# The KAN's input product in narrow pieces with copies by transfers, and the rotated query by transfers between partitions

## The chip, the core and the metric

The kernel runs on one core of a Trainium2 chip. The metric is the time of one execution on the device in microseconds; of several runs the median is taken. TensorE is called PE here, VectorE DVE, ScalarE ACT, GpSimd POOL, and SP is the engine that issues most transfers.

## What is computed

The input `x` is 16 batches (rows) of 512 tokens of 128 numbers. Two layers are applied. The first is a macaron layer of half a KAN feed-forward, attention, and half a KAN again; the second is half a mixture of experts, a linear recurrence, and half a mixture of experts again. What matters here is the first layer:

```python
# KAN: 64 input features, each with 16 hidden units of its own
s = jnp.einsum('btd,dm->btm', x, Win) + bin_
h = jax.nn.relu(s[..., None] * W1 + b1)
g = jnp.einsum('btmh,mh->btm', h, W2) + b2
out = jnp.einsum('btm,md->btd', g, Wout) + bout
...
# attention: 16 query heads of 8 numbers, 4 key heads, causal
q = q * cos + rotate_half(q) * sin
k = k * cos + rotate_half(k) * sin
...
x = x + 0.5 * kan(layernorm(x)); x = x + attn(layernorm(x)); x = x + 0.5 * kan(layernorm(x))
```

`rotate_half` swaps the two halves of a head's 8 numbers and negates one. The KAN runs twice for each batch, 32 times in all, and the query projection 16 times.

## The kernel before

**The order is written out by hand.** PE, ACT, DVE and POOL run their instructions in the order in which the program emits them (L222). The emission goes in turns. A batch b has a period of 44 turns (4 groups of heads by 11 banks, `TURNS`, L1182). In each turn the main work takes one step of `weights(b)` (L699: scores again, exp on ACT at L715, a causal mask on POOL at L717) and one of `maxima(b + 1)` (L638: scores on PE at L652, their row maxima on DVE at L657 and L662). Beside it, side work is emitted as far as the room of the turn allows (`MOST`, L234): `outputs` (L723, the product with the values at L738), `stage_in(b + 4)` (the first KAN and `attn_in`), `stage_out(b - 1)` (output product, second KAN, `gated`), and in later batches the routing. A piece of side work is a generator; each `yield` passes it to the next turn. PSUM tiles of the main work turn through 5 banks (L627), those of side work through 2 (`bank`, L259). Before batch 0 there is a ramp in which `filling[0]` is true and nothing is paced. After batch 15 the experts run (`experts`, L960), 3 turns for each of 256 jobs. SP is not in this hand-written order: its queue is laid out by the framework, near the order of emission, and it issues strictly in that queue's order, waiting at the head of it.

**The KAN** (`kan`, L347). The normalised input is transposed to `xT` (128 features by 512 tokens). Its input product is needed 4 times, since four hidden units are worked on at a time, one on each group of 32 partitions. The weights `win` hold each half (32 of the 64 features) 4 times, so that one product of 128x512 for a half (L356) makes the 4 copies at once; ACT copies each of the two results from PSUM to SBUF (L359). Then 8 ReLUs follow on ACT (L375, v = 0 to 3 for each half), and 8 narrow products of 32 output rows each (L385), which land in 4 groups of 32 partitions of one bank.

**The query** (`attn_in`, L435). `wq` gives the query, and `wqr`, its columns with the halves of each head swapped, gives the rotated query by a second product. DVE multiplies one with cos and one with signed sin (L444, L450), POOL adds them (L465). Three bf16 parts are made (`parts`, L406), written to DRAM (L425) and read back spread over partitions (L514); keys go the same way (L432, L508). `maxima` of that batch reads them first.

Of the kernel before, what the change touches and what calls it, by code (L numbers as in the profile page):

```python
# [8 lines left out]
F32 = mybir.dt.float32  # L9
# [29 lines left out]
LATE = 28  # L39
EP = 5  # L40
# [8 lines left out]
def tile_macaron(  # L49
# [55 lines left out]
    with ExitStack() as ph:  # L105
# [5 lines left out]
        hp = ph.enter_context(tc.tile_pool(name="p1_h", bufs=8))  # L111
# [66 lines left out]
        wq = cst.tile([D, NH, HD], F32, name="wq")  # L178
        nc.sync.dma_start(out=wq, in_=wq_in.rearrange("k (h d) -> k h d", d=HD))
# [6 lines left out]
        nc.sync.dma_start(out=rope, in_=rope_in)  # L186
# [8 lines left out]
        wqr = cst.tile([D, NH, HD], F32, name="wqr")  # L195
# [47 lines left out]
        def take(**work):  # L243

            for e, w in work.items():
                room[e] -= w
# [10 lines left out]
        held, kan_held, hurry = [0], [0], [False]  # L257
# [10 lines left out]
        def freed():  # L268
            held[0] -= 1
# [77 lines left out]
        def kan(b):  # L347

            _, xT = yield from norm(x[b])
            sk = []  # L350
            for half in range(2):
                while half and kan_held[0]:
                    yield
                kan_held[0] |= half
                ps = yield from bank([P, S], F32, "ps_s", 0.9)
                nc.tensor.matmul(ps, lhsT=win[:, half, :, :].rearrange("d i m -> d (i m)"), rhs=xT,  # L356
                                 start=True, stop=True)
                sh = (w1p if half else w2p).tile([P, S], F32, name=f"kan_s{half}")
                later.append(lambda sh=sh, ps=ps: nc.scalar.copy(sh, ps))  # L359
                yield  # L360
                take(act=0.6)
# [36 lines left out]
            for c in range(NT):  # L398
                nc.tensor.matmul(po[:, c, :], lhsT=gT[:, bass.ts(c, P)], rhs=wout, start=True, stop=True)  # L399
            later.append(lambda: nc.vector.tensor_add(x[b], po, x[b]))  # L400
# [20 lines left out]
        def spread(part, heads, name):  # L421

            scr = tc.dram_tile([3, HD, heads, S], BF16, name=name)
            for i in range(3):
                nc.sync.dma_start(out=scr[i].rearrange("d h t -> h d t"), in_=part[:, i, :])  # L425
            return scr
# [8 lines left out]
        def attn_in(b, st):  # L435
# [3 lines left out]
            tb = w1p.tile([P, S], F32, name="rope_b", tag="yT")  # L439
# [3 lines left out]
            nc.tensor.matmul(pa, lhsT=wq.rearrange("k h d -> k (h d)"), rhs=xT, start=True, stop=True)  # L443
            later.append(lambda: nc.vector.tensor_mul(ta, pa, rope[:, 0, :]))  # L444
            yield
            take(dve=0.7)
            freed()
            pb = yield from bank([P, S], F32, "ps_pb", 0.9)
            nc.tensor.matmul(pb, lhsT=wqr.rearrange("k h d -> k (h d)"), rhs=xT, start=True, stop=True)
            later.append(lambda: nc.vector.tensor_mul(tb, pb, rope[:, 1, :]))  # L450
            yield
            take(dve=0.7)
            freed()
# [10 lines left out]
            yield from need(pool=1.25)  # L464
            nc.gpsimd.tensor_tensor(ta, ta, tb, ALU.add)  # L465
# [18 lines left out]
            st["va"] = va  # L484
            if paced[0]:
                yield
# [17 lines left out]
            N = 3 * HD  # L504
            while taken[0] < NR * (b - NKP + 1):
                yield
# [34 lines left out]
        def prepare():  # L541
# [25 lines left out]
            centered(psc[:, 0, :], wq.rearrange("k h d -> k (h d)"))  # L567
# [4 lines left out]
            nc.vector.tensor_copy(wqr[:, :, 0:hh], wq[:, :, hh:HD])  # L572
            nc.vector.tensor_copy(wqr[:, :, hh:HD], wq[:, :, 0:hh])
# [196 lines left out]
        def stage_out(b, st):  # L770
            while len(st["out"]) < NR:
                yield
            if paced[0]:
                yield
                yield
            yT = yield from turned(st["y"].rearrange("p c r g d -> p c (r g d)"), "yT", w1p)
            po = yield from bank([P, NT, D], F32, "ps_o", 0.9)
            for c in range(NT):
                nc.tensor.matmul(po[:, c, :], lhsT=yT[:, bass.ts(c, P)], rhs=wo, start=True, stop=True)
            later.append(lambda: nc.vector.tensor_add(x[b], po, x[b]))  # L780
# [530 lines left out]
```

## Time and profile before

| | |
|---|---|
| median of 3 runs | 1580.87 us (1578.59 to 1582.71) |
| the profiled execution | 1578.82 us, of which the profile's span is 1577.0 us |
| granted TensorE clock, mean | 0.985 |
| batch periods 0 to 15 | from 108.5 us to 907.7 us of the span |
| length of the periods of batches 4 to 8 | 54.1, 48.7, 53.8, 48.7, 53.8 us |
| input product L356, 64 products in 128 records | PE, 654 ns a record |
| its copies L359 | ACT, 64 of 587 ns |
| second query product L449, 16 products in 32 records | PE, 628 ns a record |

An fp32 product appears as two records. Matmuls overlap in the pipeline, so the duration of a record is longer than what a product costs; the cost is read from the start of one group of products to the start of the next. Periods were found from the records of L715, of which there are 44 in each. A row of the profile's waits names who waited, for whom, how many microseconds in all, how often, and the longest. In the rows that split the span into stretches, the columns are the stretch, its length, and then for PE, PE's weight loads, DVE, ACT and POOL the busy time (and the count of instructions), then the granted clock, the share of DMA time and GB/s.

### The profile page before, as it was taken

How to read it: one execution, taken by the hardware profiler on the slowest of the kernel's cores; microseconds unless marked ns; L12 is line 12 of the kernel's file. 1: busy time of each engine (PE TensorE's matmuls, PEld its weight loads, DVE VectorE, ACT ScalarE, POOL GpSimd, SP SyncE). 2: the span in 40 equal slices, each digit the busy share in tenths (PEclk: the TensorE clock that was granted, in tenths of full speed). 3: DMA queues.
4: the chain of work that ended last, by engine and by line, in shares of the span. 5: the costliest groups of instructions: out<-in, count | busy, mean ns of one | idle time of the engine just before them, and what ended most of it. 6: DMA issues, size and time to landing. Idle time of an engine off the chain costs nothing.

```text
span 1577.0 us, 33209 instructions
## 1 busy us (share of the span) xinstructions
PE 1480.0 (94%) x11889; PEld 1044.6 (66%) x11905; DVE 1085.1 (69%) x3574; ACT 960.5 (61%) x1852; POOL 923.8 (59%) x1439
## 2 busy tenths in 40 slices
PE   5679999999999999999999899999999999999997
PEld 2334454445445454444444489999998999999997
DVE  5587877878788788888888245865579665753333
ACT  3455767778788777777776865444454444544443
POOL 2535545556655564556454766667666666767773
PEclk8889999999999999999999999999999999999999
DMA  5220110122111210221031113222332233333332
GB/s 136 78 62 29 58 53 14 49 59 60 32 37 54 60 52 14 56 61 41 26 91 53 52 45 71 58 61 70 73 72 61 71 73 62 81 65 68 68 68 61
DMA packets 107467, 92.89 MB, mean 59 GB/s; under 512 B 23469, under 2 KB 95862, under 8 KB 107062
## 3 DMA queue, kind: packets, MB, share of 16 engines
q1 hardware_dynamic: 84464, 67.67, 15.0%
q0 software_dynamic: 21584, 22.89, 7.8%
q8 instruction: 94, 1.54, 0.4%
q14 instruction: 71, 0.58, 0.1%
q10 hardware_dynamic: 1254, 0.20, 0.1%
HBM read 59.20 MB, written 35.45 MB: 60 GB/s over the span
## 4 chain that ended last, share of the span: by engine, by line
PE 78%; DVE 11%; ACT 4%; issue 2%; POOL 1%; DMA 1%; SPq 1%; ACTq 0%; DVEq 0%; POOLq 0%
PE ps_h L1025 14%; PE ps_y L1038 14%; PE ps_av L738 9%; PE ps_st L712 7%; PE ps_sc L652 6%; PE acc L989 5%; DVE below L657 4%; PE ps_kg L385 4%; PE ps_s L356 3%; PE ps_t L336 3%; ACT pt L715 2%; PE ps_x L954 2%; PE ps_g L799 2%; ACT kan_h L375 1%; PE ps_ko L399 1%
## 5 line engine op out<-in xcount | busy, mean ns | idle before, releaser
L715 ACT ACTIVATE pt<-ps_st 128x512 f32<-128x512 f32 (+1 forms) x704 | 378.9, 567 | 127.2 <-PE ps_st L712 115.4
L717 POOL TENSOR_SCALAR_AFFINE_SELECT pt<-pt 128x128 f32<-128x128 f32 (+2 forms) x704 | 252.5, 367 | 315.2 <-ACT pt L715 309.1
L657 DVE CUSTOM_DVE_ANT_0 below<-ps_sc,causal 128x512 bf16<-128x512 f32 (+1 forms) x512 | 315.5, 616 | 102.1 <-PE ps_sc L652 86.2
L934 POOL DMA_INDIRECT xg<-xnd,tokI x256 | 253.0, 988 | 80.8 <-issue 36.4
L1027 ACT ACTIVATE mo<-ps_h 128x512 f32<-128x512 f32 x256 | 152.8, 597 | 217.3 <-PE ps_h L1025 215.2
L1025 PE MATMUL ps_h<-xin,mw 128*128 128x128 f32 x2048 | 272.5, 276 | 0.0
L1038 PE MATMUL ps_y<-mw,mo 128*128 128x128 f32 x2048 | 270.8, 275 | 0.0
L712 PE MATMUL ps_st<-qp,kp 128*128 128x512 bf16 (+3 forms) x1008 | 247.3, 301 | 24.7 <-DVE topped L657 18.6
L652 PE MATMUL ps_sc<-kp,qp 96*128 96x512 bf16 (+3 forms) x1024 | 255.0, 303 | 10.5 <-ACT pt L715 6.6
L1025 PEld LDWEIGHTS ps_h<-xin,mw 128*128 128x128 f32 x2048 | 250.3, 192 | 12.4 <-issue 9.9
L1038 PEld LDWEIGHTS ps_y<-mw,mo 128*128 128x128 f32 x2048 | 249.4, 192 | 1.0 <-DVE ye L1035 0.8
L712 PEld LDWEIGHTS <-kp 128*128 128x128 bf16 x1024 | 94.9, 100 | 191.3 <-issue 171.5
L375 ACT ACTIVATE kan_h<-kan_s,rbias,kw 128x512 f32<-128x512 f32 x256 | 207.5, 820 | 0.0
L1055 POOL DMA_INDIRECT sum<-mo,tokI x93 | 151.5, 1629 | 72.2 <-issue 15.9
L738 PE MATMUL ps_av<-pt,va 128*32 128x512 f32 (+3 forms) x2048 | 165.4, 440 | 1.4 <-POOL pt L717 1.2
L662 DVE TENSOR_REDUCE topped<-ps_sc 128x2 f32<-128x512 f32 (+1 forms) x192 | 127.0, 682 | 23.2 <-PE ps_sc L652 22.6
L652 PEld LDWEIGHTS <-qp 96*128 96x128 bf16 x1024 | 95.5, 98 | 67.2 <-issue 40.7
L738 PEld LDWEIGHTS ps_av<-pt,va 128*32 128x32 f32 x2048 | 53.4, 109 | 87.7 <-issue 44.2
L310 POOL TENSOR_TENSOR ln_rstd<-ln_rstd,mhalf 128x4 f32<-128x4 f32 x96 | 102.3, 1066 | 8.0
L309 POOL TENSOR_SCALAR ln_rstd<-ln_mv 128x4 f32<-128x4 f32 x96 | 22.1, 230 | 135.4 <-DVE ln_mv L307 134.5
L1044 DVE SCALAR_TENSOR_TENSOR ye<-ps_y,gainT,ye 128x128 fp32r<-128x128 f32 x83 | 29.0, 349 | 84.2 <-ACT ye L1041 84.0
L1044 DVE SCALAR_TENSOR_TENSOR parts<-ps_y,gainT,parts 128x128 fp32r<-128x128 f32 x80 | 27.9, 349 | 83.9 <-ACT parts L1041 83.8
(202 smaller groups left out, 2279.4 us busy)
## 6 DMA issues: line engine op xcount, KB each, us to landing
qp<-qs SPq DMA_DIRECT2D x64, 288.0 KB
xnd<-kan_x SPq DMA_DIRECT2D x32, 256.0 KB
sum<-x SPq DMA_DIRECT2D x62, 128.0 KB
qs<-qpart SPq DMA_DIRECT2D x48, 128.0 KB
kp<-ks SPq DMA_DIRECT2D x48, 96.0 KB
x<-in_L_attn_x_dram SPq DMA_DIRECT2D x16, 256.0 KB
mw<-in_L_ffn_w_dram SPq DMA_DIRECT2D x16, 256.0 KB
xg<-xnd,tokI POOLq DMA_INDIRECT x256, 2.5
```

Source lines behind the costliest of these rows:

```text
L375: nc.scalar.activation(h, sk[half], AF.Relu, bias=rbias[:, half, v : v + 1], scale=kw1[:, half, v : v + 1])
L652: nc.tensor.matmul(v[:, u, 0:n], lhsT=qp[r][0:MXR, g, bass.ts(c, P)], rhs=kp[0:MXR, r, 0:n], start=alone, stop=(u == len(gs) - 1), skip_gr ...
L657: nc.vector.tensor_tensor_reduce(below[:, 0:n], v[:, 0, 0:n], causal[:, S - n : S], 1.0, LOWEST, ALU.add, ALU.max, accum_out=maxs[:, h, c ...
L712: nc.tensor.matmul(v[:, u, 0:n], lhsT=kp[ROWS, r, bass.ts(c, P)], rhs=qp[r][ROWS, g, c * P : S], start=True, stop=True)
L715: nc.scalar.activation(o, v[:, :, 0:n], AF.Exp, scale=HD ** -0.5)
L717: nc.gpsimd.affine_select(out=dg, in_=dg, compare_op=ALU.is_ge, fill=0.0, base=0, pattern=[[0, len(gs)], [1, P]], channel_multiplier=-1)
L738: nc.tensor.matmul(po[32 * g : 32 * g + 32, c * P : S], lhsT=va[:, c, r, :], rhs=pt[:, g, OFF[c] : OFF[c] + n], start=(c == 0 and not odd) ...
L934: nc.gpsimd.indirect_dma_start(out=xgs[i // E % 2][:, i % E, :], out_offset=None, in_=xnd[b], in_offset=bass.IndirectOffsetOnAxis(ap=tokI[ ...
L1025: nc.tensor.matmul(pst[:, f, :], lhsT=mw1[e][:, bass.ts(f, P)], rhs=xins[i // E % 2][:, i % E, :], start=True, stop=True)
L1027: nc.scalar.activation(hs[u], pst, AF.Gelu)
L1038: nc.tensor.matmul(py, lhsT=hs[u][:, f, :], rhs=mw2[e][:, f, :], start=(f == 0), stop=(f == NF - 1))
L1055: nc.gpsimd.indirect_dma_start(out=sums[k, b], out_offset=bass.IndirectOffsetOnAxis(ap=tokI[g][:, n : n + 1], axis=0), in_=added[b % 2 * ( ...
```

## The change

- **KAN.** Where `filling[0]` is false, the product is made once: four narrow products, each 32 features by 256 tokens (L380 of the changed kernel), land in the four groups of 32 partitions of one bank of 128x256 (two halves of the features by two halves of the tokens). ACT copies that bank once (`kan_m`). Two transfers write it to DRAM (L391), and two transfers read each half of the features back 4 times over, as 128x512 (L402). Between them the generator passes 4 turns, and another 6 (`REST`) before the first ReLU. Where `filling[0]` is true, the two wide products stay.
- **Two KANs may be under way at once** (`kan_held` counts to 2); their ReLUs are served in the order of tickets. `kan_s0` and `kan_s1` have two buffers each. The last hidden unit of each half is written over `kan_s`, so that `kan_h` has 6 buffers and not 8, and `gT` over `kan_s0`.
- **Query.** The columns of `wq` are kept by the number within the head first, so that the two halves of all heads are partitions 0 to 63 and 64 to 127. Past the ramp the second product is left out: DVE multiplies the query with sin into `unturned` (which uses `qpart`'s space) and with cos, and two transfers of 64 partitions exchange the halves (L516). POOL's addition comes at least 4 turns later. `rope` is loaded by 4 transfers that repeat 4 rows 16 times, and not by one.
- **`yT` and `rope_b` share a buffer**, so a lock `y_held` keeps `stage_out` and `attn_in` apart there. The reads of keys and queries come 3 turns after the writes.

In the changed program 27 of the 32 KANs and 13 of the 16 queries go the new way. The turns are the same in both programs: 44 in each period, the experts begin at turn 821, and the end is turn 1610.

```diff
-        nc.sync.dma_start(out=wq, in_=wq_in.rearrange("k (h d) -> k h d", d=HD))
+        nc.sync.dma_start(out=wq.rearrange("k d h -> k (d h)"), in_=wq_in)
...
-        nc.sync.dma_start(out=rope, in_=rope_in)
+        halves = [slice(a * P // 2, (a + 1) * P // 2) for a in range(2)]
+        for a in range(2):
+            for w in range(2):
+                rows = a ^ w
+                src = rope_in[rows * HD // 2 : (rows + 1) * HD // 2, w, :]
+                nc.sync.dma_start(out=rope[halves[a], w, :], in_=src.unsqueeze(1).to_broadcast([HD // 2, NH, S]))
...
-            for half in range(2):
-                while half and kan_held[0]:
-                    yield
-                kan_held[0] |= half
-                ps = yield from bank([P, S], F32, "ps_s", 0.9)
-                nc.tensor.matmul(ps, lhsT=win[:, half, :, :].rearrange("d i m -> d (i m)"), rhs=xT,
-                                 start=True, stop=True)
-                sh = (w1p if half else w2p).tile([P, S], F32, name=f"kan_s{half}")
-                later.append(lambda sh=sh, ps=ps: nc.scalar.copy(sh, ps))
...
+            direct = filling[0]
...
+            else:
+                ps = yield from bank([P, S // 2], F32, "ps_s", 0.75)
+                for half in range(2):
+                    for th in range(2):
+                        o = th * M + half * MH
+                        nc.tensor.matmul(ps[o : o + MH, :], lhsT=win[:, half, 0, :],
+                                         rhs=xT[:, th * S // 2 : (th + 1) * S // 2], start=True, stop=True)
+                once = w1p.tile([P, S // 2], F32, name="kan_m")
+                later.append(lambda: nc.scalar.copy(once, ps))
+                yield
+                take(act=0.4)
                 freed()
-                sk.append(sh)
-            yield
-
+                yield
+                scr = tc.dram_tile([2, MH, S], F32, name=f"kn{len(kns)}")
+                kns.append(scr)
+                for th in range(2):
+                    nc.sync.dma_start(out=scr.rearrange("a m t -> (a m) t")[:, th * S // 2 : (th + 1) * S // 2],
+                                      in_=once[th * M : (th + 1) * M, :])
+                for _ in range(4):
+                    yield
+                while kan_held[0] == 2:
+                    yield
+                kan_held[0] += 1
+                mine_ = tickets[0]
+                tickets[0] += 1
+                for half in range(2):
+                    sh = w2p.tile([P, S], F32, name=f"kan_s{half}")
+                    nc.sync.dma_start(out=sh, in_=scr[half].unsqueeze(0).to_broadcast([NI, MH, S]))
+                    sk.append(sh)
+                for _ in range(REST):
+                    yield
+
+            while serving[0] < mine_:
+                yield
...
-                h = hp.tile([P, S], F32, name="kan_h")
+                h = sk[half] if v == NV - 1 else hp.tile([P, S], F32, name="kan_h")
...
-            gT = w2p.tile([P, S], F32, name="kan_g", tag="kan_s0")
+            gT = sk[0]
             later.append(lambda: nc.scalar.copy(gT, pg))
-            kan_held[0] = 0
+            serving[0] += 1
...
-            pb = yield from bank([P, S], F32, "ps_pb", 0.9)
-            nc.tensor.matmul(pb, lhsT=wqr.rearrange("k h d -> k (h d)"), rhs=xT, start=True, stop=True)
-            later.append(lambda: nc.vector.tensor_mul(tb, pb, rope[:, 1, :]))
...
+            else:
+                while y_held[0]:
+                    yield
+                y_held[0] = True
+                unturned = qpart.rearrange("p i t -> p (i t)")[:, 0 : 2 * S].bitcast(F32)
+                later.append(lambda: nc.vector.tensor_mul(unturned, pa, rope[:, 1, :]))
+                yield
+                take(dve=0.7)
+                yield from need(dve=0.7)
+                nc.vector.tensor_mul(ta, pa, rope[:, 0, :])
+                freed()
+                tb = w1p.tile([P, S], F32, name="rope_b", tag="yT")
+                for a in range(2):
+                    nc.sync.dma_start(out=tb[halves[a], :], in_=unturned[halves[1 - a], :])
...
+            if not direct:
+                for _ in range(4):
+                    yield
+                yield from need(pool=1.25)
+                nc.gpsimd.tensor_tensor(ta, ta, tb, ALU.add)
+                y_held[0] = False
+                yield
...
             qs = spread(qpart, NH, f"qs{b}")
             N = 3 * HD
+            for _ in range(3 if paced[0] else 0):
+                yield
```

More of the change, by code (lines that the diff above doesn't have):

```diff
@@ L39 @@
 LATE = 28
+REST = 6
 EP = 5
@@ L194, in tile_macaron @@
         hh = HD // 2
-        wqr = cst.tile([D, NH, HD], F32, name="wqr")
+        wqr = cst.tile([D, HD, NH], F32, name="wqr")
         identb = cst.tile([P, P], BF16, name="identb")
@@ L364, in kan @@
-            yield
+                kan_held[0] += 1
+                mine_ = tickets[0]
+                tickets[0] += 1
+                sk = [w2p.tile([P, S], F32, name=f"kan_s{half}") for half in range(2)]
+                for half in range(2):
+                    ps = yield from bank([P, S], F32, "ps_s", 0.9)
+                    nc.tensor.matmul(ps, lhsT=win[:, half, :, :].rearrange("d i m -> d (i m)"), rhs=xT,
+                                     start=True, stop=True)
+                    later.append(lambda half=half, ps=ps: nc.scalar.copy(sk[half], ps))
+                    yield
+                    take(act=0.6)
+                    freed()
@@ new lines, in kan @@
+                yield
+            else:
[9 more added lines that the diff above has]
+                take(act=0.4)
+                freed()
+                yield
[6 more added lines that the diff above has]
+                    yield
+                while kan_held[0] == 2:
+                    yield
+                kan_held[0] += 1
+                mine_ = tickets[0]
+                tickets[0] += 1
+                for half in range(2):
+                    sh = w2p.tile([P, S], F32, name=f"kan_s{half}")
[3 more added lines that the diff above has]
+                    yield
@@ L463, in attn_in @@
             yield
-            yield from need(pool=1.25)
-            nc.gpsimd.tensor_tensor(ta, ta, tb, ALU.add)
+            if direct:
+                yield from need(pool=1.25)
+                nc.gpsimd.tensor_tensor(ta, ta, tb, ALU.subtract)
+                y_held[0] = False
             take(dve=0.4)
@@ L484, in attn_in @@
             st["va"] = va
+            if not direct:
+                for _ in range(4):
+                    yield
+                yield from need(pool=1.25)
+                nc.gpsimd.tensor_tensor(ta, ta, tb, ALU.add)
+                y_held[0] = False
+                yield
             if paced[0]:
```

47 lines of the change are left out of this document (31 added, 16 removed).

## The prediction

> **What bounds the kernel now.** I read the busy shares first, then the slices, then PE's own waits, then the stretches by batch, and last the start times of PE's groups. Of the page, parts 1 and 2:
>
> ```profile
> PE 1480.0 (94%) x11889; PEld 1044.6 (66%) x11905; DVE 1085.1 (69%) x3574; ACT 960.5 (61%) x1852; POOL 923.8 (59%) x1439
> ...
> PE   5679999999999999999999899999999999999997
> ...
> DVE  5587877878788788888888245865579665753333
> ACT  3455767778788777777776865444454444544443
> ```
>
> PE is at nine tenths from slice 4 on (one slice and the last excepted), in the attention stage (to about 908 us) as in the experts; DVE and ACT stand at seven to eight in the attention stage. The page warns that a busy PE is not a PE at its peak, so its waits have to say it. Of PE's waits from 300 to 900 us, the two longest:
>
> ```profile
> PE ps_st L712 <- DVE topped L657: 11.1, 28, 0.8
> PE ps_sc L652 <- ACT pt L715: 6.5, 14, 0.8
> ```
>
> In 600 us PE waited 11 us for DVE and 6.5 for ACT, always for a free bank and never longer than 0.8 us. So PE's own work sets the pace, with short hand-overs. How firmly, the stretches by batch period tell (period 4, 5, 6, 13 and 14):
>
> ```profile
> 308.60:362.70 54.10, 52.16 (x424) 27.07 (x425) 42.65 (x139) 41.21 (x77) 30.12 (x65) 1.00 0.16 45
> 362.70:411.40 48.70, 47.00 (x373) 24.33 (x373) 39.91 (x136) 40.04 (x75) 29.18 (x61) 1.00 0.17 49
> 411.40:465.20 53.80, 51.84 (x423) 26.88 (x424) 42.33 (x139) 40.53 (x76) 29.87 (x64) 1.00 0.15 45
> ...
> 778.60:825.50 46.90, 43.22 (x362) 22.76 (x362) 40.41 (x135) 32.91 (x63) 25.00 (x57) 1.00 0.23 66
> 825.50:870.60 45.10, 41.82 (x347) 21.68 (x349) 36.24 (x121) 32.61 (x62) 18.78 (x50) 1.00 0.23 70
> ```
>
> All have the same 44 turns of main work; periods 13 and 14 lack side work. This is a natural experiment on what a microsecond of PE is worth. Periods 4 to 8 are 51.8 us long on average with 50.0 us of PE. Period 13: 4.9 us shorter for 6.8 us less PE, 0.72. Period 14: 6.7 for 8.2, 0.82. Period 1 (44.9 long, 42.2 of PE): 6.9 for 7.8, 0.88. I take **0.8**, the middle.
>
> **PE's saving.** The granted clock is 1.00 here, so start times show prices. Of PE's order in time, columns start, length, instruction:
>
> ```profile
> 460.23 1.02 PE L443 MATMUL ps_pa<-kan_xT,wq 128*128 128x512 f32 x2
> 461.09 0.38 PE L712 MATMUL ps_st<-qp,kp 128*128 128x256 bf16 x2
> ...
> 461.64 1.02 PE L449 MATMUL ps_pb<-kan_xT,wqr 128*128 128x512 f32 x2
> 462.50 0.39 PE L712 MATMUL ps_st<-qp,kp 128*128 128x128 bf16 x4
> ...
> 463.26 0.64 PE L457 MATMUL ps_kv<-kan_xT,wk 128*32 128x128 f32 x16
> 463.83 1.08 PE L461 MATMUL ps_kv<-wv,kan_xT 128*128 128x32 f32 x8
> ```
>
> From start to next start, a wide fp32 product of 512 columns costs 0.86 us (460.23 to 461.09, 461.64 to 462.50); L356 is the same form. The new narrow products have no row, but L457 is their sister: 8 products of 32 output rows by 128 columns, in four groups of partitions, take 0.57 us. Four products by 256 columns move the same columns in each group, so I take 0.57. The bounds: 0.43 (half of 0.86, all four side by side at no overhead) and 1.72 (one after the other).
>
> - KAN, 27 times: two wide products out (1.72), one narrow set in (0.57): 1.15 each, 31.0 us.
> - Query, 13 times: one wide product out: 0.86 each, 11.2 us.
>
> Together 42.2 us less on PE; by the bounds 46.0 or 11.2. Times 0.8 this is **33.7 us** of time. One of the KANs (batch 15's second) runs in the expert stage, where PE is equally full; I don't price it apart.
>
> **ACT, DVE, POOL.** ACT loses 54 copies of 587 ns (L359) and gains 27 of 128x256, which the copies of that form at L956 put at 367: 21.8 us less. It was not the bound, so this is no term; it is cover for the case that ACT would come next. DVE keeps its two multiplications (681 ns each) and POOL its addition. What is late next when PE's work goes is DVE: in period 11 (672.7 to 725.7, with routing) it is busy 44.9 of 53.0 us. The 0.72 to 0.88 above holds DVE's short waits already.
>
> **The transfers.** Added are 54 writes, 54 reads and 26 exchanges, 134 issues on SP. SP's rows give 0.33 us to 0.82 us an issue, so 44 to 110 us over the stage, in a queue that stands waiting for hundreds (226 us for L686 alone). Bytes: a KAN moves 128 KB out and 512 KB in, a query 256 KB, about 20.6 MB over 800 us or 26 GB/s on top of 45 to 49. Neither is on the path so long as the data land in time. That is the question for three deadlines:
>
> ```profile
> SPq L425 <- ACT qpart L409: 140.1, 14, 23.7
> SPq L693 <- DMA ms<-mr: 37.8, 25, 3.9
> ```
>
> ```profile
> 478.01 0.82 SPq L514 DMA_DIRECT2D qp<-qs  x1
> ```
>
> The first fence holds waits of SP (for whom, total, times, longest), the second a line of SP's order in time: the issue alone of a 288 KB read holds SP for 0.82 us.
>
> *ReLU.* From the write's emission to the first ReLU lie 4 + 6 turns of 51.8/44 = 1.18 us, after the gain about 1.1: 11 us. Needed: two issues (0.7), landing in DRAM 1.5 (the wait for `ms`, 37.8/25), an issue of the read 0.7, and its landing. The nearest row is L514, 288 KB: in the trace's packets the one issued from 489.25 to 490.01 begins at 490.8 and ends at 493.0, 3.0 us behind its issue. Sum 5.9 us; with the second read queued behind the first, about 9, and that half is read two ReLUs later. It is hidden; the bound, if the read's 128 packets of 2 KB (84 ns each, the rows of that size) went one behind another, is 10.8 us and a stall of some 3 us at each KAN.
>
> [...]
>
> *Rotated query.* The exchange of 64 partitions has the addition at least 6 turns behind it; issue and landing need about 3 us of 6.6. Hidden.
>
> *Scores.* `attn_in` ends later. In the emission order the reads of a batch's queries stand 9 turns (batches 10, 14, 15) to 20 turns ahead of the first score that uses them, where it was 27 to 43. From the last key write (477.11) to the end of the third key read's issue took 4.2 us for batch 9, landing 3 more, and the writes run about 2 turns behind their emission: some 8 turns. For batch 10 two reads of the KAN stand ahead of the queries in SP's queue. So this edge is tight: 0 to 10 us in all, I take **2**, as only three batches come near.
>
> *Ramp.* `rope` takes 3 more issues, about 1 to 2 us of SP, but SP then waits until 12.9 us for ACT's `ropek`, and DVE is busy with memsets when the rows of x arrive. 0 to 2 us, I take **0.5**.
>
> **Sum.** 1578.8 (profiled execution, span 1577.0 and 1.8 around it) - 33.7 + 2 + 0.5 = **1548 us**. That execution lies 2 us below the median shown; by the median it would be 1550. By the ends: all 42.2 passes, nothing late, 1537; a PE microsecond worth 0.72 and 12 us of lateness, 1560.
>
> **Rivals.**
>
> 1. *The gain is half eaten by DVE and late queries.* For: DVE is at 85% in period 11, and if it can't pass the 86% of period 13, periods 9 to 12 gain about 1 us each and not 2.5; scores lose 20 turns of slack. Price: 6 us and 6 to 12 us. Time about 1562. Against: PE's waits for DVE are 0.8 us at most.
> 2. *Slower: `kan_s` comes late.* SP issues in order, and it has stood up to 23.7 us behind one wait (L425 for `qpart`); a KAN's read behind such a wait makes the ReLU late, ACT stands, exp stands behind it in ACT's queue, and PE for want of banks. It decides when write to landing exceeds 11 us by 33.7/27 = 1.25 us at every KAN. At 2.5 us over, 67 us are lost: about 1612. Against: in the new SP queue the reads mostly stand in the order of emission, not behind later writes; the exception is batch 13, whose read follows expert weights that wait for a group of heads.
> 3. *The narrow products don't run side by side* (1.72 a set): only the query's 11.2 x 0.8 remain, about 1572. Against: L457.
> 4. *Nothing*, late data and gains cancel: 1580.
>
> **Chances.** Forecast (1536 to 1556) 0.62; better still 0.05; rival 1 (1556 to 1570) 0.16; rival 3 0.03; rival 4 0.04; rival 2 0.10. The measurement can tell about 0.3% (4.7 us) from no change. Faster 0.86, same 0.04, slower 0.10. The range 1536 to 1575 takes in the forecast, rival 1 and rival 3; it leaves out rivals 2 and 4 and the best case, 0.19.
>
> **What would show it.** Right: the narrow sets 0.57 us from start to start; periods 4 to 8 near 49 us with about 47 us of PE; ACT idle before the ReLUs below 0.1 us each; PE's waits for `qp` a few microseconds. Wrong: ReLUs or POOL's addition waiting for a DMA; PE's idle time in a period above 4 us; PE waiting at the first score of a batch; a first score later than about 71 us in the ramp (L652 begins at 68.7 us).

## The result, and the profile after

The changed kernel takes 1591.91 us (median of 4 runs, 1589.35 to 1593.12), the kernel before 1581.51 us beside it: a ratio of 1.0072, with a 95% interval of 1.006 to 1.0084. It is slower; the forecast was 1548 us, and slower had a chance of 0.10. The profiled execution took 1593.12 us, its span is 1591.4 us (1577.0 before).

The page of the changed kernel, parts 1 and 2:

```profile
PE 1452.9 (91%) x11987; PEld 1031.9 (65%) x11987; DVE 1079.6 (68%) x3574; ACT 940.6 (59%) x1825; POOL 918.1 (58%) x1439
...
PE   5679989899999988899878799999999999999997
...
DVE  5588887888888868888768245855669665753333
ACT  3446676778777757787656855444454444544443
...
PEclk9879999999999989999989999999999999999999
```

PE works 27 us less than before (1480.0), yet the span is 14 us longer: PE's row now has eights and sevens in the attention stage, and PEclk dips at two of them (the slices around 577 and 816 us). So PE's time was saved, and PE stands.

The price of the narrow set was as forecast. Of PE's order in time (start, length, instruction, idle time before it), from 460.76 to 461.33 are 0.57 us:

```profile
460.76 0.64 PE L380 MATMUL ps_s<-kan_xT,win 128*32 128x256 f32 x8 [0.35 <-ACT kan_xT L345]
461.33 0.39 PE L786 MATMUL ps_st<-qp,kp 128*128 128x256 bf16 x2
```

**Where the time went.** The whole attention stage and the whole expert stage in one row each, before:

```profile
108.50:907.80 799.30, 750.43 (x5949) 382.90 (x5964) 626.74 (x2076) 599.24 (x1122) 440.21 (x953) 0.99 0.16 47
907.80:1577.00 669.20, 659.07 (x5618) 629.34 (x5616) 387.86 (x1290) 320.04 (x667) 442.95 (x412) 0.99 0.30 66
```

and after:

```profile
114.90:911.00 796.10, 716.42 (x6038) 366.65 (x6037) 624.18 (x2078) 574.95 (x1088) 432.88 (x951) 0.98 0.25 73
911.00:1591.40 680.40, 663.08 (x5626) 631.51 (x5626) 385.09 (x1290) 323.14 (x672) 444.31 (x415) 0.99 0.30 66
```

Length less PE's busy time is PE's idle time: 48.9 us before, 79.7 after in the attention stage. In the trace the clock is either full or half (a granted share of 1.00 or 0.50), and the records of one transpose (L343 of the changed kernel) begin 0.109 us apart at full clock and 0.213 at half. Of the time that PE is busy at half clock, half is lost: 6.7 us before and 12.7 after in this stage (a stretch at half clock that falls into a wait costs nothing there). Busy time less that is PE's work at full clock, an estimate, since the ends of matmuls are modelled. The account of the 14.4 us:

| us | before | after | difference |
|---|---|---|---|
| ramp, to the first exp of batch 0 | 108.5 | 114.9 | +6.4 |
| attention stage, PE's work at full clock | 743.6 | 703.7 | -39.9 |
| attention stage, lost to half clock while busy | 6.7 | 12.7 | +6.0 |
| attention stage, PE idle, waits over 1.7 us | 4.6 | 24.1 | +19.5 |
| attention stage, PE idle, shorter waits | 44.2 | 55.6 | +11.4 |
| expert stage | 669.3 | 680.4 | +11.1 |

The saving is there: 39.9 us in this stage, where the forecast has 41.1 (42.2 less the one KAN that runs in the expert stage). The shorter waits take 11.4 of it, a share of 0.29; the forecast left 0.2 for them. The rest is eaten by a few long waits and by what follows them. PE's largest kinds of wait in this stage (for whom, total, times, longest), before:

```profile
PE ps_st L712 <- DVE topped L657: 16.7, 39, 0.8
PE ps_sc L652 <- ACT pt L715: 6.6, 15, 0.8
```

and after, from 120 to 910 us:

```profile
PE ps_sc L726 <- ACT pt L789: 24.6, 28, 8.0
PE ps_st L786 <- DVE topped L731: 13.9, 37, 0.8
...
PE ps_sc L722 <- ACT pt L789: 5.6, 9, 1.9
PE ps_sc L726 <- DMA kp<-ks: 4.5, 2, 4.0
```

All waits of PE for DVE over 0.15 us together did not grow (32.7 us before, 32.9 after). The growth is in waits for ACT (10.9 us before, 36.9 after) and for one transfer. Eight waits are longer than 1.7 us, 24.1 us in all: three stand behind late data (4.0, 2.7 and 8.0 us), five, of 1.8 to 2.0 us each, have another cause, which comes below. The worst is in period 13. SP's order there:

```profile
811.20 2.01 SPq L391 DMA_DIRECT2D kn<-kan_m  x2
813.32 0.86 SPq L588 DMA_DIRECT2D qp<-qs  x1
814.61 2.14 SPq L582 DMA_DIRECT2D kp<-ks  x3
816.80 2.42 SPq L588 DMA_DIRECT2D qp<-qs  x3
819.27 1.14 SPq L402 DMA_DIRECT2D kan_s<-kn  x2
```

and ACT's:

```profile
817.33 0.60 ACT L789 ACTIVATE pt<-ps_st 128x512 f32<-128x512 f32 x1 [0.21 <-PE ps_st L786]
828.27 0.81 ACT L418 ACTIVATE kan_h<-kan_s,rbias,kw 128x512 f32<-128x512 f32 x1 [10.35 <-DMA kan_s<-kn]
```

and PE's:

```profile
829.62 0.59 PE L726 MATMUL ps_sc<-kp,qp 96*128 96x512 bf16 x1 [8.04 <-ACT pt L789]
```

The KAN's read is issued behind seven reads of keys and queries (1.4 MB, 5.9 us of issues) and lands 8 us after its issue. The ReLU stands at the head of ACT's queue for 10.35 us, the exps behind it, and PE waits 8.04 us for a bank. The clock falls to half 2.0 us after the start of this wait and comes back 4.2 us after its end, so that 2.1 us are lost on top. In the rows of these stretches the mean clock is in the third column from the end:

```profile
821.60:823.60 2.00, 0.00 (x0) 0.00 (x0) 0.19 (x1) 0.00 (x0) 0.00 (x0) 1.00 0.76 217
823.60:829.60 6.00, 0.00 (x0) 0.00 (x0) 0.00 (x0) 1.32 (x3) 0.00 (x0) 0.50 0.68 203
829.60:833.80 4.20, 4.01 (x27) 1.25 (x26) 2.25 (x8) 2.94 (x5) 2.32 (x5) 0.50 0.77 209
```

Rows of whole periods (5, 9 and 13) show waits and clock together:

```profile
353.40:403.00 49.60, 46.42 (x405) 24.14 (x404) 40.74 (x137) 38.69 (x74) 29.56 (x63) 1.00 0.24 72
556.70:616.80 60.10, 51.43 (x413) 26.25 (x414) 43.34 (x138) 37.28 (x73) 26.11 (x58) 0.91 0.23 68
767.20:829.00 61.80, 48.59 (x389) 24.84 (x388) 44.21 (x151) 33.15 (x64) 26.00 (x59) 0.90 0.24 75
```

Period 9 took 50.9 us before. In it PE waits for batch 10's keys, whose reads stand behind the KAN's in SP's queue:

```profile
544.73 1.15 SPq L402 DMA_DIRECT2D kan_s<-kn  x2
...
546.89 2.06 SPq L582 DMA_DIRECT2D kp<-ks  x3
```

```profile
559.23 0.58 PE L726 MATMUL ps_sc<-kp,qp 96*128 96x512 bf16 x1 [4.02 <-DMA kp<-ks]
```

The half clock around this wait costs another 2.5 us, and a second stretch of it, from 591.5 us, 7 us after one of the five other waits, 1.7.

### The profile page after: what moved, and what is told of

Same layout as the page of the kernel before. It is cut to its first block, busy times and chain, and to the rows that moved or that the text cites. A ratio compares the mean times of both kernels' runs of the same rounds, so it can differ in the third digit from the quotient of the medians.

```text
span 1591.4 us, 33597 instructions
## 1 busy us (share of the span) xinstructions
PE 1452.9 (91%) x11987; PEld 1031.9 (65%) x11987; DVE 1079.6 (68%) x3574; ACT 940.6 (59%) x1825; POOL 918.1 (58%) x1439
## 5 line engine op out<-in xcount | busy, mean ns | idle before, releaser
L791 POOL TENSOR_SCALAR_AFFINE_SELECT pt<-pt 128x128 f32<-128x128 f32 (+2 forms) x704 | 246.9, 358 | 335.7 <-ACT pt L789 329.2
L726 PE MATMUL ps_sc<-kp,qp 96*128 96x512 bf16 (+3 forms) x1024 | 258.2, 306 | 31.3 <-ACT pt L789 24.6
L786 PE MATMUL ps_st<-qp,kp 128*128 128x512 bf16 (+3 forms) x1024 | 255.7, 304 | 21.2 <-DVE topped L731 13.9
L812 PE MATMUL ps_av<-pt,va 128*32 128x512 f32 (+3 forms) x2048 | 169.7, 450 | 0.8 <-POOL pt L791 0.8
L418 ACT ACTIVATE kan_h<-kan_s,rbias,kw 128x512 f32<-128x512 f32 x192 | 155.1, 816 | 17.8 <-DMA kan_s<-kn 17.8
L343 PE MATMUL ps_t<-ident,kan_x 128*128 128x128 f32 x384 | 62.7, 290 | 27.0 <-DVE kan_x L331 20.6
```

The lines of the kernel that those rows point to most:

```text
L726: nc.tensor.matmul(v[:, u, 0:n], lhsT=qp[r][0:MXR, g, bass.ts(c, P)], rhs=kp[0:MXR, r, 0:n], start=alone, stop=(u == len(gs) - 1), skip_gr ...
L786: nc.tensor.matmul(v[:, u, 0:n], lhsT=kp[ROWS, r, bass.ts(c, P)], rhs=qp[r][ROWS, g, c * P : S], start=True, stop=True)
L791: nc.gpsimd.affine_select(out=dg, in_=dg, compare_op=ALU.is_ge, fill=0.0, base=0, pattern=[[0, len(gs)], [1, P]], channel_multiplier=-1)
L812: nc.tensor.matmul(po[32 * g : 32 * g + 32, c * P : S], lhsT=va[:, c, r, :], rhs=pt[:, g, OFF[c] : OFF[c] + n], start=(c == 0 and not odd) ...
```

## Experiments

The theory at the start (A) was: the saving is real; a few late transfers, each with half clock behind it, the ramp's `rope` loads and the start of the experts give it back. Every ratio is to the kernel before, with its 95% interval.

### The two halves

```diff
# kan_alone, in attn_in             # query_alone, in kan
-            direct = filling[0]
+            direct = True
```

> Only the KAN's half of the change; the query is made by two products everywhere, as before (L515 not taken), with the new layout of its columns and the 4 loads of rope kept. Theory A (the saving on PE is real, a few late transfers with the half clock behind them, the ramp and the start of the experts give it back): 27 x 1.15 x 0.8 = 25 us gained, the ramp's 6.4 us stay, the queries stand 12 to 24 turns ahead (9 to 20 in the full change), so that one or two stalls of some 8 us remain: 1565 to 1580. Rival B (the KAN's way by DRAM costs everywhere, by hand-overs and by two KANs under way): no better than the full change, 1585 or more, with periods of 50 us and more. Rival C (the query's half does the harm): 1581 - 25 + 6 = 1562 or less.

> Only the query's half of the change; the KAN keeps its two wide products everywhere. Theory A: 13 x 0.86 x 0.8 = 9 us gained, the ramp's 6.4 us stay, queries stand 22 to 28 turns ahead, so no stall and no half clock between 120 and 900 us: 1578 (1573 to 1583). Rival B (the harm is the KAN's alone): the same 1578. Rival C (the query's half does the harm): 1588 or more, with PE idle for over 2 us at the first score of some batches.

`kan_alone` took 1582.95 us (0.9998, 0.9983 to 1.0014; its ten runs lie between 1576.7 and 1588.4): no change, above theory A's range and below rival B's. `query_alone` took 1596.51 us (1.0085, 1.0062 to 1.0107). Theory A had 1578 for the latter and is wrong there: no read was late, PE had 9 us less work in the attention stage (734.8), and still it was idle for 67.8 us (48.9 before). The time is rival C's, but not its sign, since no wait at a first score is over 2 us. Something besides late data costs time. What grew are PE's waits for DVE, 49.1 us in all (32.7 before), none of those shown over 1.2 us:

```profile
PE ps_m L746 <- DVE topped L736: 8.9, 9, 1.2
PE ps_kv L520 <- DVE rope_a L512: 7.2, 8, 1.2
```

The second row is the new pair of multiplications, which holds the bank that PE needs next.

### Neither half, and its lock

```diff
# neither: both of the edits above; neither_lock: also
-                while kan_held[0] == 2:
-                    yield
-                kan_held[0] += 1
...
                 for half in range(2):
+                    while half and kan_held[0]:
+                        yield
+                    if half:
+                        kan_held[0] += 1
```

> The change's bookkeeping alone: the KAN keeps its wide products and the query its two products everywhere, but the new layout, the 4 rope loads, 6 buffers for kan_h with the ReLU in place, two KANs under way, the lock on yT and the 3 turns before the reads stay. The query's half alone cost 14 us over periods 2 to 12 although PE had 9.5 us less to do there. Theory E (this comes from the exchange's own form: two multiplications one behind the other on DVE, whose bank PE needs next): periods 2 to 12 as before, 581 us in all, the whole 1582 + 5 of the ramp = 1587 (1584 to 1590). Rival F (it comes from the bookkeeping, which shifts side work so that it falls on DVE and POOL at worse moments): periods 2 to 12 at 595 us or more, the whole 1600 or more.

> As the bookkeeping alone (wide products for the KAN, two products for the query, everywhere; 1591.8 us), but with the lock of the kernel before: the second half of a KAN's product waits until the KAN ahead has finished its ReLUs, so that only one KAN and a half is under way. Theory H (two KANs under way shift the ramp and the periods): the ramp ends at 109 to 111 us instead of 112.5, periods 2 to 12 at 581 instead of 584.6, the whole 1584 (1581 to 1587). Rival (the layout, the 4 rope loads, the 3 turns and the lock on yT do it): 1589 or more.

`neither` took 1591.83 us (1.0067, 1.005 to 1.0084), as much as the full change, with no work saved. That is just above theory E's range and far below rival F's. PE's waits for DVE are 29.3 us here and 49.1 in `query_alone`, so that E's cause, the multiplications on DVE, fits what the query's half adds; no run changes them alone. `neither_lock` took 1581.20 us (1.0005, 0.9995 to 1.0015), as much as the kernel before: theory H holds. So with wide products, letting two KANs be under way costs 10.6 us (9.8 by the two ratios), and layout, `rope` loads, 3 turns and the lock on `yT` nothing that can be told. The profiles of the two differ in the ramp (112.5 and 109.2 us) and in periods 2 to 12 (584.6 and 579.5). The four medians are then a square: 1591.8 with neither half, 1596.5 with the query's, 1583.0 with the KAN's, 1591.9 with both. From there the KAN's half gains 9 or 5 us and the query's loses 5 or 9.

### The ramp

```diff
# rope_one, ramp_order: the table in the new order, made on the host
-        for a in range(2):
-            for w in range(2):
...
+        nc.sync.dma_start(out=rope, in_=ropeq_in)
# ramp_order: also
             while serving[0] < mine_:
                 yield
+            for _ in range(2 if direct and mine_ else 0):
+                yield
```

> The full change with the table of rope laid out on the host for the new order and loaded by one transfer instead of 4 that repeat rows. Theory A (these loads cause the later start of period 0, 114.9 for 108.5 us): period 0 starts at 109 us again, 6 us less than the changed kernel, 1586 (1583 to 1588). Rival (the later start comes from something else in the ramp, such as the order of the KANs or the subtraction on POOL): period 0 stays at 114 us or later, 1590 to 1593.

> The full change with rope loaded by one transfer, and 2 turns more before the ReLUs of every KAN of the ramp but the first, which puts ACT's instructions of the ramp into the order that they had before (the copy to qpart of batch 1 ahead of the copy to gT of batch 2). The one load alone gave 1.9 of the 6.4 us. Theory G (the order in ACT's queue is the rest): period 0 starts at 108.5 to 109.5 us. Rival (the rest is PE's clock or POOL): 112 us or later. The whole follows by as much: 1586, or 1592.

`rope_one` took 1596.34 us (1.0085, 1.0058 to 1.0111), above both ranges; its period 0 begins at 113.0 us, 1.9 before that of the changed kernel. This does not show that the loads cost anything: with the four loads, period 0 begins at 112.5 us in `neither`, 113.2 in `query_alone` and 115.6 in `kan_early`, whose ramps are the changed kernel's. `ramp_order` took 1594.83 us (1.0096, 1.0073 to 1.0119) with period 0 at 114.3 us: theory G falls, for this way of restoring the order. Two turns more bring ACT's order nearer to that of before, but a later copy to `gT` now comes behind the issues of `ms`, which go through ACT's queue in the ramp, and waits 9.5 us. What the ramp loses depends on the lock, as `neither_lock` shows: it keeps the four loads, its order on ACT in the ramp is that of the kernel before, and its period 0 begins at 109.2 us.

### The end of the stage

```diff
# kan_actq
-                    nc.sync.dma_start(out=sh, in_=scr[half]...
+                    nc.scalar.dma_start(out=sh, in_=scr[half]...
# kan_early, slack_early: in kan
+            direct = filling[0] or now[0] > 690
# slack_early: also IN = 36, and without the 3 turns before the reads
# rest_late
-                for _ in range(REST):
+                for _ in range(16 if 690 < now[0] < 821 else REST):
```

> The full change with the reads of kan_s issued from ACT's queue and not from SP's. Theory A (the reads are late because they stand behind 7 issues and 1.4 MB of key and query reads on SP's queue): the waits of the ReLUs at 772, 829 and 910 us go, and the half clock behind them; 54 issues of 0.55 us on ACT are 30 us more of an engine at 6 tenths, as many as the change took from it: 1570 to 1582. Rival D (the reads wait for their write to land, or the engines of the transfers are full): the ReLUs' wait moves to ACT's issue, ACT stands in front of exps more often than before: 1592 or more.

> The full change, but KANs from turn 690 on (the second KANs of batches 12 to 15) keep the wide products. Theory A (the late kan_s reads of these four stretch periods 13 to 15 by 15 us and the start of the experts by most of 11): period 13 at 47 us instead of 61.8, the experts' stage at 671 instead of 680, PE pays 4 x 1.15 us: 1573 (1568 to 1578). Rival (the loss at the end is general, not these reads'): 1588 or more.

> The full change, but from turn 690 to 821 a KAN passes 16 turns and not 6 between its read and its first ReLU. Nothing is moved to PE. Theory A (the ReLUs come before the data, that is all that is wrong at the end): the waits at 772, 829 and 910 us are gone, periods 12 to 15 and the experts lose what the four wide products gained in kan_early: 1574 (1570 to 1580). Rival J (the reads also hold up keys and queries, or the later second KANs hold up the experts): the wait moves to the scores or to the experts, 1584 or more.

> As kan_early, and the 3 turns before the reads of keys and queries left out and the input stage begun at turn 36 of a period instead of 38; in the emission the reads then stand 16 to 27 turns ahead of the first score in batches 5 to 14 (9 to 20 before), 9 only in batch 15. Theory A: the wait of 4 us for batch 10's keys and the half clock behind it go, period 9 at 51 us instead of 60: 1564 (1560 to 1570). Rival (DVE and the hand-overs are the limit, the wait only hides it): no faster than kan_early.

`kan_actq` took 1593.17 us (1.0073, 1.0044 to 1.0102): in the range of rival D. The ReLU's wait at the end of period 13 is 6.5 us and no longer 10.35, another 2.6 us moved to the issue in ACT's queue, so SP's queue was a part of the lateness and not the whole.

`kan_early` took 1574.68 us (0.9954, 0.9938 to 0.9971), `rest_late` 1577.77 us (0.9986, 0.9973 to 0.9999): 17 and 14 us less than the changed kernel. The second does not touch PE's work; it lets the ReLUs come later. That the ReLU comes before its data is thus the cause at the end, for 14 us of the whole, and period 13 went from 61.8 to 54.4 and 52.0 us (forecast 47 for the former). Period 13 of `rest_late`:

```profile
765.10:817.10 52.00, 46.26 (x375) 24.23 (x374) 42.12 (x145) 32.47 (x62) 25.98 (x59) 0.93 0.18 51
```

The experts' stage came back with the wide products (672.0) and not with the longer rest (678.6). From the start of period 13 to the end the two take 808.0 and 810.6 us, the changed kernel 824.2 and the kernel before 798.4.

`slack_early` took 1581.20 us (0.9998, 0.9984 to 1.0012). Period 9 did fall to 50.3 us, as theory A said, but periods 13 to 15 rose from 135.9 to 147.1 us: with the input stage elsewhere, another batch's keys (at 813 us) were late. The time is as the rival had it. Earlier alone is no cure.

### Versions that keep the old lock in the ramp

```diff
# best_kan and best_both: rope_one's load, kan_early with the lock of the
# kernel before where filling[0] is true, without the 3 turns; in attn_in
+            direct = True                                    # best_kan
+            direct = filling[0] or b in (10, 13, 14, 15)     # best_both
```

> Narrow KANs only from the end of the ramp to turn 690, with the lock of the kernel before in the ramp, rope in one load, the query by two products everywhere, no 3 turns before the reads. Theory (the KAN's saving of 22 x 1.15 us on PE is real; ramp, end and the start of the experts are as before): the ramp ends at 109 us, periods 2 to 12 take 565 to 570 us, periods 13 to 15 129 to 132, the experts 671: 1567 (1561 to 1573). Rival (the gain came from the query's half, as periods 2 to 12 were 5 us shorter with it): 1575 or more.

> As best_kan, and the query by one product with the exchange in batches 3 to 9, 11 and 12; batches 10, 13, 14 and 15, whose reads were late, keep two products. In the emission the reads stand 15 turns or more ahead of the first score. Theory (with no read late, the query's half is worth its PE time too): no wait of PE above 2.5 us from 120 to 890 us, periods 2 to 12 at 556 to 562 us, the whole 1560 (1554 to 1568) and faster than best_kan. Rival I (the exchange costs more on DVE and POOL than the product on PE, as it did alone): slower than best_kan by 3 us or more.

`best_kan` took 1572.68 us (0.9945, 0.9926 to 0.9964), within its range; `best_both` 1573.54 us (0.9951, 0.9933 to 0.9969), 14 above its forecast. The query's half saved 9 us of PE's work at full clock (719.8 to 711.1) and gained nothing, but it is not 3 us slower either, as rival I had it.

### What the query's half costs in the full change: a shared buffer

In five periods of the changed kernel PE stands for 1.8 to 2.0 us at one place. PE, POOL and ACT there:

```profile
474.90 0.27 PE L722 MATMUL ps_sc<-causal,identb 128*128 128x256 bf16 x1 [1.89 <-ACT pt L789]
```

```profile
472.58 1.26 POOL L554 TENSOR_TENSOR rope_a<-rope_a,rope_b 128x512 f32<-128x512 f32 x1
```

```profile
472.13 0.82 ACT L418 ACTIVATE kan_h<-kan_s,rbias,kw 128x512 f32<-128x512 f32 x1
473.87 0.58 ACT L345 COPY yT<-ps_t 128x512 f32<-128x512 f32 x1 [0.93 <-POOL rope_a L554]
474.35 0.99 ACT L789 ACTIVATE pt<-ps_st 128x384 f32<-128x384 f32 x2
```

`yT` is written where `rope_b` was, so the copy waits for POOL's addition, and the exp stands behind the copy. The kernel before shares this buffer too (both tiles have the tag `yT`), and there no copy to `yT` waits for POOL: what is new is that the addition comes later. In `query_alone` one copy waits so, for 0.9 us; the buffer is not what costs time there.

```diff
# own_rest: rest_late with, own_both: best_both with, at both places,
# and kcr in the space of bout to make room
-                tb = w1p.tile([P, S], F32, name="rope_b", tag="yT")
+                tb = w1p.tile([P, S], F32, name="rope_b")
```

> As rest_late (1577.8 us), but rope_b has a buffer of its own and doesn't share yT's; the order of every engine's instructions is the same. In rest_late PE stands five times for 1.8 to 2.0 us, at the same place of periods 6, 7, 9, 10 and 11 (423, 473, 582, 635 and 689 us), each time for an exp on ACT, and in the changed kernel the exp there stands behind the copy to yT, which waits for POOL's addition that still reads rope_b. Theory K (the shared buffer is the cause): the five waits go, 9 us, and with them the half clock behind two of them, 3 us: 1566 (1563 to 1571). Rival L (ACT is late from the ReLUs of two KANs one behind the other): the waits stay, 1575 or more.

> As best_both (1573.5 us), with the buffer of its own for rope_b. Theory K: the waits of 1.9 us at 422, 472 and 635 us go, those of 4.1 and 3.8 us at 556 and 765 stay: 1566 (1562 to 1570). Rival L: 1572 or more.

`own_rest` took 1572.02 us (0.9942, 0.9925 to 0.9959), `own_both` 1569.67 us (0.9919, 0.9903 to 0.9936): 5.8 and 3.9 us less than with the shared buffer (7 and 5 by the ratios). All five waits are gone, and the half clock behind two of them; theory K holds for the waits, while `own_rest` gained half of the 12 us forecast and lies 1 us above its range. Beside `best_kan` the query's half now gains 3 us, which is within the intervals. Of ACT in `own_rest`, at the same place:

```profile
468.88 0.82 ACT L418 ACTIVATE kan_h<-kan_s,rbias,kw 128x512 f32<-128x512 f32 x1
469.58 0.59 ACT L345 COPY yT<-ps_t 128x512 f32<-128x512 f32 x1
470.05 1.00 ACT L789 ACTIVATE pt<-ps_st 128x384 f32<-128x384 f32 x2
```

### All of it, and the reads in another order of rows

```diff
# all_fixed: the buffer, the one load and the ramp's lock, and in kan
+            direct = ramp or now[0] > 780
+                for _ in range(16 if now[0] > 690 else REST):
# in attn_in
-            for _ in range(3 if paced[0] else 0):
+            for _ in range(3 if paced[0] and b != 10 else 0):
# read16 (in the changed kernel) and read16_fixed (in all_fixed): win, w2d,
# kw1, kb1, bin_ laid out with the copy i behind the feature m, and
-    in_=scr[half].unsqueeze(0).to_broadcast([NI, MH, S]))
+    in_=scr[half].unsqueeze(1).to_broadcast([MH, NI, S]))
```

> The full change with every cure found so far: a buffer of its own for rope_b, rope in one load, the lock of the kernel before in the ramp, 16 turns between read and ReLU from turn 690 on, wide products only for KANs that begin after turn 780, and no 3 turns before the reads of batch 10. Theory (the changed kernel's loss is the sum of these five causes): against own_rest 3 to 5 us less in the ramp, 6 less in the experts and up to 7 less in period 9: 1553 (1547 to 1562). Rival M (PE's saved time is lost in hand-overs wherever the large waits go): 1564 or more.

> The changed kernel (1591.9 us), but the four copies of a KAN's hidden feature lie on neighbouring partitions (feature first, copy second), so that the read of kan_s walks 32 rows of the scratch, each repeated 4 times, where it walked 4 repetitions of 32 rows. Bytes, packets and issues are the same. In the read ahead of batch 10's keys the 2 KB packets come 91 in 2 us, at 84 ns each 3.8 at a time, and the keys' packets come behind them. Theory N (the reads run on 4 of the 16 transfer engines, and what is queued there behind them is late): some 15 at a time, the waits at 557, 772, 829 and 910 us shrink from 4.0, 2.7, 8.0 and 4.2 us to below 2 and their half clock with them: 1576 (1570 to 1582). Rival O (SP's issue time and the bytes are what makes them late): 1587 or more.

> As all_fixed (1568.1 us), with the same order of partitions for the KAN's copies. There the wait for batch 10's keys was still 3.6 us and period 9 was 60.3 us long. Theory N: that wait goes, period 9 takes 50 to 52 us, the whole 1558 (1554 to 1563). Rival O: period 9 stays above 57 us, 1566 or more.

`all_fixed` took 1568.06 us (0.991, 0.9894 to 0.9927), 15 above its forecast and in the range of rival M. But a long wait is left: the ramp is back (108.3 us), and period 9 is still 60.3 us long; the keys of batch 10 were issued at 537.9 us and waited for until 549.5. In the trace the packets of the KAN's read went ahead of theirs, 91 of 2 KB in 2 us, each of 84 ns: 3.8 at a time.

`read16` took 1584.52 us (1.0014, 1.0001 to 1.0027), 7 less than the changed kernel, between theory N and rival O. The 256 packets of 2 KB of the same read now begin within 2.2 us, where it was 8.1 in the changed kernel (over all 27 KANs the median is 2.2 us, and was 5.9), and the wait for keys at 557 us is gone: period 9 takes 55.4 us and not 60.1. Who waited for the read (ACT's ReLU: us, times), in the changed kernel:

```profile
  ACT kan_h L418: 17.8, 10
```

and in `read16`:

```profile
  ACT kan_h L418: 12.2, 2
```

Eight of ten waits go; the two long ones (4.1 and 8.1 us), behind 1.4 MB of other reads, stay. That is O's part.

`read16_fixed` took 1559.19 us (0.9855, 0.9835 to 0.9875), as forecast (1558), and is the best version: 22 us below the kernel before and 33 below the changed one. The wait for batch 10's keys is gone, as theory N said, but period 9 takes 54.6 us, between N's 50 to 52 and rival O's 57:

```profile
545.60:600.20 54.60, 49.14 (x412) 25.24 (x412) 44.30 (x144) 37.32 (x72) 27.57 (x61) 0.97 0.24 70
```

Its attention stage and PE's largest kinds of wait in it:

```profile
108.50:884.50 776.00, 713.46 (x6040) 365.06 (x6038) 622.95 (x2076) 579.02 (x1097) 435.05 (x953) 1.00 0.26 74
```

```profile
PE ps_st L790 <- DVE topped L735: 13.8, 35, 0.8
PE ps_sc L730 <- ACT pt L793: 12.1, 26, 2.9
```

Waits over 1.7 us are 4.6 us in all, as before the change, and 3.3 us are lost to half clock. Of 33.5 us less work (743.6 to 710.1) the stage is 23.3 us shorter: 0.70. The whole gain lies ahead of period 13: from period 0 to there it takes 639.4 us where it was 670.1, and from there to the end 809.8 where it was 798.4.

## Why the prediction was wrong, point by point

- **The price of a narrow set: right.** 0.57 us from L457, 0.569 to 0.573 measured at 25 of the 27 sets; the 41.1 us forecast for the attention stage became 39.9.
- **0.8 of it passes: near what was measured, but not shown by what it was read from.** Short waits took 11.4 of 39.9 us, which leaves 0.71, and 0.70 was left in the best version. The natural experiment compared periods without a long wait, and in them other engines had less to do too (ACT 32.9 us in period 13, 40 to 41 in periods 4 to 8), while the change took its time from PE and ACT. Of PE's waits the prediction read two rows; from 300 to 900 us there was also one of 2.5 us, for the normalised input at 888 us. The long waits needed terms of their own.
- **The failing step: "Neither is on the path so long as the data land in time", with 2 us for all lateness.** In most KANs the 11 us ahead of the ReLU were enough. What I left out is the company: the KAN's read behind seven reads of keys and queries (period 13), and the keys behind the KAN's read (period 9). The prediction names the second order and takes 2 us for it; the first it does not name. The row read for the landing ends at 493.2 us and not at 493.0, which changes nothing. The measured price is 14 to 17 us at the end (`rest_late`, `kan_early`) and 5 to 6 us in period 9 (60.1 to 55.4 with `read16`, 60.3 to 54.6 with `read16_fixed`).
- **The order of the read's rows.** 3.8 packets of the read at a time in the old order, and with 32 rows outermost 7 to 9 us less time in two kernels. I asked only whether the ReLU is in time, by the landing of another read (3.0 us, L514), and kept the sum. The packets of a KAN's two reads began within 5.9 us at the median in the changed kernel, and within 2.2 in `read16`. Their price was paid by whoever was queued behind.
- **Two KANs under way: described in the change and not priced.** 10.6 us (`neither` against `neither_lock`). I counted on the turns being the same in both programs; they are, and the order within them is not.
- **The shared buffer: described too, and not priced.** 5.8 and 3.9 us. It was shared before; now POOL's addition is later, and a wait on ACT for it delays the exps behind it.
- **Ramp 0.5 us, experts none.** They were +6.4 and +11.1. With the old lock the ramp is as before (109.2 us with the four loads of `rope`, 108.3 to 110.7 with one). At the start of the experts' stage PE waits 4.1 us for ACT's copy to `xin`, which stands behind a late KAN's ReLUs, and later 2.4 us for a gather, each with half clock; with wide products in the last batches the stage takes 672 us (`kan_early`).
- **Rival 1** named DVE as the next bound: in the full change PE's waits for DVE did not grow, with the query's half alone they did (49.1 us). **Rival 2** named the right mechanism (the read behind SP's queue, ReLU, exp, banks), but as a delay at every KAN; ten ReLUs waited, two of them long.

What stays open: why two KANs under way cost 5 us in periods 2 to 12 with nothing late (PE waits 13.9 us for ACT's exps from the ramp to the experts against 8.9 with the lock, 17.8 against 22.6 for DVE's maxima, none over 0.8 us); why period 9 takes 54.6 us with no wait for keys; and why the stretch from period 13 to the end takes 808 to 811 us in `kan_early`, `rest_late` and all later versions but `read16` (798.4 before), even in `best_kan` (809.6), which has wide products and two query products there.

## What to carry to other kernels

Before costing a new transfer at nothing, write out the queue it joins: what stands ahead of it, and what already there will now stand behind it, in issues and in bytes; and of a repeated read, measure both orders of its dimensions: here 32 rows outermost, each repeated 4 times, in place of 4 repetitions of 32 rows took 7.4 and 8.9 us off (`read16`, `read16_fixed`). An order of work that is laid out by hand is part of the price of a change: run the change's bookkeeping alone (here 10.6 us), and look for shared buffers whose last reader now comes later. Here a PE that is busy at 94% passed on seven tenths of what was taken from it, once no new wait was longer than 3 us.

## What the runs showed of the hardware

A wait of PE can cost more than its length. In the changed kernel eight waits of 1.9 us and more follow the start of period 0. At six of them the clock falls to half, 1.8 to 3.4 us after the wait's start, for 3.4, 6.8 or 10.2 us. What of such a stretch falls into the wait costs nothing, so that the 10.2 us at the longest wait cost 2.1 and the six cost 1.4 to 3.1 us each on top. In the attention stage all time lost to half clock is 12.7 us in the changed kernel and 3.3 in the best version. A wait of 1.89 us was enough at 473 us; one of 1.90 us at 423 us and one of 2.00 us at 690 us were not, and no run shows what decides it.
